# A graph-attention edge loop on one core: node parts and weights made two groups ahead, pairs weighed one pair ahead of TensorE

## The chip, the cores and the metric

The kernel runs on one core of a Trainium2 chip. The metric is the device time of one execution in microseconds, as the median of several runs without a profiler. Apart from these, one execution was recorded by the hardware profiler; all views come from that one.

## What is computed

Four graph layers on 4096 nodes with 512 features and 65536 edges (src, dst); each normalises, applies a relu, runs the layer and adds its result to x. The change lies in layer 0, a graph attention with 8 heads of 64 features:

```
h = einsum('nc,hcf->hnf', x, W)
e = s_src[:, :, None] + s_dst[:, None, :]
e = where(e > 0, e, 0.2 * e);  e = where(adj, e, NEG_INF)
att = softmax(e, axis=-1)
out = einsum('hij,hjf->hif', att, h)     # then softmax over the 512 features
```

adj has every edge once and the diagonal. The kernel doesn't build the 4096 x 4096 matrix. It goes over the edges, sorted by source: for each edge it gathers the destination's row of h (512 numbers) and 8 scores, makes a weight exp(...) for each of the 8 heads, and adds weight times row to the source node, together with the weight itself (the softmax's denominator) and a one (the degree, which layer 1 needs).

## The kernel before

**Stages.** The program sorts the edges and projects the nodes (to about 240 us of the profile), then runs layer 0's edge loop (`attend`), layer 1's edge loop (rows of ytab, from about 1190 us), layer 2's edge network (about 2080 to 4670 us), a node update, and layer 3's edge loop (rows of ztab, from about 5190 us). The three plain edge loops each issue 512 indirect gathers of 128 rows from GpSimd's queue (L412).

**A group.** `attend` works on 64 groups of 8 tiles of 128 edges. For a group g these are the steps, with the engine that runs them:

- `fetch` (GpSimd, L412): 8 indirect gathers into `rows[g]`, which has four buffers. The first gather of group g+3 waits until the sums of group g-1 have left its buffer.
- `one_hots` (DVE, L407): a 128 x 128 matrix for each tile that says which source node (within a window) an edge belongs to.
- `turn` (TensorE, L623): the 8 one-hots transposed into PSUM (`t_ps`).
- `turned` (ACT L631, two casts to bfloat16; ACT L635 and DVE L636, which blend the node parts of the two node blocks of the window into `of`). The blocks' numbers are read into registers by L418 first, on ACT's and on DVE's queue.
- `source_parts` (TensorE, L644): 8 small products that give each edge its source's part of the score (`e_ps`, a single buffer).
- `scores` (DVE L650, L652, L653, L654, L656: sum of three parts, add the gathered part, leaky relu, subtract the source's own top, clamp; ACT L657 exp and L658 ones).
- `weights` (DVE L664: weight times a mark that drops repeated edges, into PSUM `w_ps`, two buffers; ACT L665 copies it beside the rows).
- `weigh_last` (ACT L672): the last two heads of two tiles are scaled, four instructions for a pair of tiles.
- `weigh` (DVE L678): the first six heads of a pair of tiles, one instruction.
- `add_up` (TensorE, L684): a pair of tiles summed into `sum_ps`; four matmuls of 261 columns, which the profile shows as eight.
- `keep` (DVE L424, twice): the window's sums added into the accumulators of two node blocks, whose numbers also come through L418.

**What sets the order.** The loop stands under a manual schedule: each engine executes in the order in which the code names its instructions, and waits where data or a buffer is missing. So the order of the calls in the loop (L693 to L728) is the order on each queue. In iteration g the sums of group g are made, group g-1 is kept, group g+1 is turned, scored and weighted, the one-hots of g+2 are made and the rows of g+3 fetched. Within iteration g a pair of tiles is weighed on DVE just ahead of its sums: pair 0, sums 0, pair 2, (keep g-1), sums 2, pair 4, one-hots, sums 4, scores of g+1, pair 6, sums 6, weights of g+1.

Of the kernel before, what the change touches and what calls it, by code (L numbers as in the profile page):

```python
# [34 lines left out]
def kernel(  # L35
# [71 lines left out]
    s_loc = src_pool.tile([P, W], F32, name="s_loc")  # L107
# [296 lines left out]
    def one_hots(pool, loc, t0, n, bufs=None, ids=None, dtype=F32):  # L404

        oh = pool.tile([P, n, P], dtype, name="oh", bufs=bufs)
        nc.vector.tensor_tensor(oh, (row_i if ids is None else ids).unsqueeze(1).to_broadcast([P, n, P]),  # L407
                                loc[:, t0:t0 + n].unsqueeze(2).to_broadcast([P, n, P]), op=OP.is_equal)
        return oh
# [7 lines left out]
    def block_of(eng, bi, t):  # L417
        return eng.value_load(bi[:, t:t + 1], min_val=0, max_val=NB - 1)  # L418
# [171 lines left out]
    GT = 8  # L590
# [4 lines left out]
    def attend(ctx):  # L595
        if True:
            ep = ctx.enter_context(tc.tile_pool(name="edge", bufs=2))
# [4 lines left out]
            ids_ps = both_ps[:, :P]  # L602
# [5 lines left out]
            def at(g):  # L608
                return g * GT

            def fetch(g):
                rows = ep.tile([P, GT, DA], F32, name="rows", bufs=4)
                for j in range(GT):
                    gather(rows[:, j, :D + H], htab, s_dst[:, at(g) + j:at(g) + j + 1])
                return rows

            def turn(oh):

                made = []
                for j in range(0, GT, 4):  # L620
                    t_ps = eps.tile([P, 4, P], F32, name="t_ps")
                    for k in range(4):
                        nc.tensor.transpose(t_ps[:, k, :], oh[:, j + k, :], ident)  # L623
                    made.append(t_ps)
                return made

            def turned(g, made):

                oh_t = ep.tile([P, GT, P], BF16, name="oh_t")
                for j, t_ps in enumerate(made):  # L630
                    nc.scalar.copy(oh_t[:, 4 * j:4 * j + 4, :], t_ps)  # L631
                of = ep.tile([P, 2, 3 * 2 * H], BF16, name="of")
                near = [node3[:, ds(block_of(e, s_bi[:, k, :], g), 1)].rearrange("p b k c -> p (b k c)")
                        for k, e in enumerate((nc.scalar, nc.vector))]
                nc.scalar.activation(of[:, 0, :], near[0], AF.Copy, scale=s_half[:, 0, g:g + 1])  # L635
                nc.vector.scalar_tensor_tensor(of[:, 1, :], near[1], s_half[:, 1, g:g + 1], of[:, 0, :],  # L636
                                               op0=OP.mult, op1=OP.add)
                return oh_t, of[:, 1, :]

            def source_parts(oh_t, of):  # L640

                e_ps = eps.tile([P, GT, 3, 2 * H], F32, name="e_ps", bufs=1)
                for j in range(GT):
                    nc.tensor.matmul(e_ps[:, j].rearrange("p k c -> p (k c)"), oh_t[:, j, :],  # L644
                                     of, start=True, stop=True)
                return e_ps

            def scores(rows, e_ps):
                near = ep.tile([P, GT, 2 * H], F32, name="near")
                nc.vector.reduce_sum(near, e_ps.rearrange("p t k c -> p t c k"), axis=AX.X)  # L650
                u = ep.tile([P, GT, H], F32, name="u")
                nc.vector.tensor_add(u, near[:, :, :H], rows[:, :, D:D + H])  # L652
                nc.vector.scalar_tensor_tensor(u, u, 0.2, u, op0=OP.mult, op1=OP.max)  # L653
                nc.vector.tensor_sub(u, u, near[:, :, H:])  # L654

                nc.vector.tensor_scalar(u, u, SAFE_RANGE + 10.0, None, op0=OP.min)  # L656
                nc.scalar.activation(u, u, AF.Exp)  # L657
                nc.scalar.copy(rows[:, :, D + H:], one2.unsqueeze(1).to_broadcast([P, GT, 2]))  # L658
                return u

            def weights(g, rows, u):

                w = w_ps[:, g % 2]
                nc.vector.tensor_mul(w, u, s_new[:, at(g):at(g) + GT].unsqueeze(2).to_broadcast([P, GT, H]))  # L664
                nc.scalar.copy(rows[:, :, D:D + H], w)  # L665

            def weigh_last(j, rows):

                two = rows[:, j:j + 2]
                for k in range(2):  # L670
                    for h in range(VH, H):
                        nc.scalar.activation(two[:, k, h * F:(h + 1) * F], two[:, k, h * F:(h + 1) * F], AF.Copy,  # L672
                                             scale=two[:, k, D + h:D + h + 1])

            def weigh(g, j, rows):

                part = rows[:, j:j + 2, :VH * F].rearrange("p t (h f) -> p t h f", h=VH)
                nc.vector.tensor_mul(part, part,  # L678
                                     w_ps[:, g % 2, j:j + 2, :VH].unsqueeze(3).to_broadcast([P, 2, VH, F]))

            def add_up(j, rows, oh, ps):
                for k in range(2):
                    for c in range(2):
                        nc.tensor.matmul(ps[:, c, :HW], oh[:, j + k, :], rows[:, j + k, c * HW:(c + 1) * HW],  # L684
                                         start=j + k == 0, stop=j + k == GT - 1)

            def keep(g, ps):
                add_window(g, s_bi, s_half,
                           lambda b: acc[:, ds(b, 1), :].rearrange("p b (c d) -> p (b c) d", c=2), ps[:, :, :HW])


            rows, ohs, sums = {}, {}, {}
            for g in range(-3, groups + 1):  # L693
                now = lambda k: 0 <= k < groups
                if now(g + 3):
                    rows[g + 3] = fetch(g + 3)
                if now(g + 1):
                    made = turn(ohs[g + 1])
                if now(g):
                    sums[g] = eps.tile([P, 2, D], F32, name="sum_ps")  # L700
                    weigh(g, 0, rows[g])
                    add_up(0, rows[g], ohs[g], sums[g])
                    weigh_last(2, rows[g])
                    weigh(g, 2, rows[g])
                if now(g - 1):
                    keep(g - 1, sums.pop(g - 1))
                    del rows[g - 1], ohs[g - 1]
                if now(g + 1):
                    parts = turned(g + 1, made)
                if now(g):  # L710
                    add_up(2, rows[g], ohs[g], sums[g])
                    weigh_last(4, rows[g])
                    weigh(g, 4, rows[g])
                if now(g + 2):
                    ohs[g + 2] = one_hots(ep, s_loc, at(g + 2), GT, 3, ids_ps)
                if now(g + 1):
                    e_ps = source_parts(*parts)
                if now(g):
                    add_up(4, rows[g], ohs[g], sums[g])
                if now(g + 1):  # L720
                    u = scores(rows[g + 1], e_ps)
                if now(g):
                    weigh_last(6, rows[g])
                    weigh(g, 6, rows[g])
                    add_up(6, rows[g], ohs[g], sums[g])
                if now(g + 1):
                    weights(g + 1, rows[g + 1], u)
                    weigh_last(0, rows[g + 1])  # L728

    one2 = node_pool.tile([P, 2], F32, name="one2")  # L730
    nc.vector.memset(one2, 1.0)
    attend()
    l0_pool.close()

# [734 lines left out]
```

## Time and profile before

| | |
|---|---|
| median of 3 runs (lowest to highest) | 5614.41 us (5613.85 to 5614.54) |
| the profiled execution's own time | 5951.3 us |
| its span, first to last instruction | 5949.5 us |
| mean granted TensorE clock | 0.951 |
| busy in the span: PE, DVE, ACT, POOL | 88%, 60%, 56%, 52% |
| layer 0's loop, 240 to 1030 us, busy: PE, DVE, ACT, POOL | 600.5, 519.7, 366.5, 484.1 of 790 us |
| in the same stretch: TensorE clock, share of DMA engines | 0.92, 0.63 |

How to read it: times in the profile are microseconds from the first instruction. PE is TensorE's matmuls, whose ends are modelled; DVE is VectorE, ACT ScalarE, POOL GpSimd. An idle time is put down to what ended it, as far as the profile can name it. Indirect gathers show as DMA_INDIRECT on POOL; [...] the rows land later.

### The profile page before, as it was taken

The numbers are of one execution on the slowest core, as the hardware profiler recorded it, in microseconds if no ns is written. First come the engines' busy times: TensorE is split into PE (matmuls) and PEld (weight loads), VectorE is DVE, ScalarE is ACT, GpSimd is POOL, SyncE is SP. The second block draws the span as 40 slices with busy tenths as digits, with TensorE's granted clock in tenths as the row PEclk, the third lists the DMA queues.
The fourth block names the chain that finished last, engine by engine and source line by source line (L and its number), as shares of the span: only waits on it lengthen the run. The fifth ranks groups of instructions, "written<-read, shape, count | busy, mean of one in ns | idle before, by whom it ended". The sixth has DMA issues, their size and how long they took to land.

```text
span 5949.5 us, 56469 instructions
## 1 busy us (share of the span) xinstructions
PE 5249.2 (88%) x17274; PEld 2791.2 (47%) x17274; DVE 3558.3 (60%) x5695; ACT 3356.1 (56%) x5015; POOL 3082.0 (52%) x2604
## 2 busy tenths in 40 slices
PE   7677777869999799999999999999999899866676
PEld 4466666424444344444444444444444666522222
DVE  8566667623223377777777777777777565522323
ACT  1144445423433488888888888888888433333333
POOL 0266664066666465665565566566554111166665
PEclk9799999989999899999999999999999999988888
DMA  3366665467777555555555555555554212266775
GB/s 105 98 176 181 184 181 159 159 212 232 234 227 232 147 118 108 111 110 109 110 111 110 108 113 109 108 112 110 108 110 84 78 64 68 84 187 187 209 222 183
DMA packets 344871, 841.72 MB, mean 141 GB/s; under 512 B 60272, under 2 KB 76656, under 8 KB 344560
## 3 DMA queue, kind: packets, MB, share of 16 engines
q0 software_dynamic: 237568, 673.35, 46.8%
q1 hardware_dynamic: 106992, 164.66, 8.1%
q8 instruction: 141, 2.31, 0.2%
q14 instruction: 170, 1.39, 0.1%
HBM read 752.62 MB, written 85.20 MB: 141 GB/s over the span
## 4 chain that ended last, share of the span: by engine, by line
PE 75%; DVE 8%; another core or an unknown queue 6%; issue 4%; ACT 3%; DMA 2%; DVEq 1%; POOL 1%; SPq 0%; POOLq 0%; ACTq 0%
PE m_ps L401 30%; PE sum_ps L768 13%; PE small_ps L967 5%; PE tr_ps L974 4%; PE sum_ps L994 4%; PE pq_ps L868 4%; PE o_ps L401 4%; PE u_ps L1177 4%; PE sum_ps L684 4%; DVE rows L678 2%; DVE acc L424 1%; PE y_ps L401 1%; ACT oh L744 1%; POOL rows L412 1%
## 5 line engine op out<-in xcount | busy, mean ns | idle before, releaser
L401 PE MATMUL m_ps<-w_sb,h_t 128*128 128x512 f32 x4096 | 1848.0, 599 | 1.5 <-ACT h_t L976 1.5
L768 PE MATMUL sum_ps<-g,oh 128*128 128x512 f32 x2048 | 1012.2, 636 | 248.2 <-ACT oh L745 133.1
L401 PEld LDWEIGHTS m_ps<-w_sb,h_t 128*128 128x128 f32 x4096 | 757.1, 190 | 1002.9 <-issue 989.1
L950 POOL DMA_INDIRECT pg<-qtab,d_dst x512 | 1050.9, 2053 | 156.5 <-issue 155.4
L412 POOL DMA_INDIRECT pg<-ptab,d_src x512 | 498.5, 974 | 909.6 <-ACT h_t L976 726.4
L768 PEld LDWEIGHTS sum_ps<-g,oh 128*128 128x128 f32 x2048 | 412.1, 205 | 793.6 <-issue 600.2
L412 POOL DMA_INDIRECT rows<-htab,s_dst x512 | 484.1, 946 | 515.8 <-issue 360.1
L424 DVE SCALAR_TENSOR_TENSOR acc<-sum_ps,d_half,acc 128x512 f32 x512 | 384.6, 751 | 581.8 <-remote 241.3
L412 POOL DMA_INDIRECT g<-ytab,s_dst x512 | 484.9, 947 | 460.8 <-issue 326.9
L684 PE MATMUL sum_ps<-rows,oh 128*128 128x261 f32 x2048 | 528.2, 408 | 160.2 <-DVE rows L678 87.1
L412 POOL DMA_INDIRECT g<-ztab,d_src x512 | 486.6, 950 | 324.5 <-issue 142.7
L424 DVE SCALAR_TENSOR_TENSOR acc<-sum_ps,s_half,acc 128x522 f32 (+1 forms) x256 | 193.6, 756 | 575.1 <-PE sum_ps L768 275.7
L684 PEld LDWEIGHTS sum_ps<-rows,oh 128*128 128x128 f32 x2048 | 392.5, 199 | 249.5 <-DVE rows L678 101.1
L976 ACT COPY h_t<-tr_ps 128x512 f32<-128x512 f32 x512 | 287.2, 588 | 338.8 <-PE tr_ps L974 314.2
L994 PE MATMUL sum_ps<-parts,oh 128*128 128x512 f32 x1024 | 344.1, 457 | 12.4 <-DVE parts L987 10.7
L868 PE MATMUL pq_ps<-w_sb,ht_mid 128*128 128x512 f32 x512 | 272.2, 619 | 58.7 <-ACT ht_mid L863 58.7
L988 DVE TENSOR_TENSOR parts<-z,parts 128x1024 fp32r<-128x1024 f32 x256 | 313.9, 1226 | 8.7
L967 PE MATMUL small_ps<-w1e,et 64*128 64x512 f32 x1024 | 295.3, 648 | 20.8 <-ACT et L959 13.0
L744 ACT ACTIVATE oh<-row_i,d_loc 128x128 f32<-128x128 f32 x512 | 162.2, 387 | 249.5 <-remote 149.1
L974 PE MATMUL tr_ps<-ident,pg 128*128 128x128 f32 x2048 | 297.4, 278 | 3.9 <-DVE pg L1070 0.6
L974 PEld LDWEIGHTS tr_ps<-ident,pg 128*128 128x128 f32 x2048 | 224.6, 142 | 118.7 <-issue 84.5
L1168 POOL TENSOR_TENSOR h_sb<-h_sb,b_bc 128x1024 f32<-128x1024 f32 x16 | 37.7, 2357 | 453.5 <-PE tr L1152 358.0
(283 smaller groups left out, 7937.7 us busy)
## 6 DMA issues: line engine op xcount, KB each, us to landing
xt<-in_x_dram SPq DMA_DIRECT2D x16, 1024.0 KB
eg<-in_edge_attr_dram SPq DMA_DIRECT2D x128, 128.0 KB
htab<-acc SPq DMA_DIRECT2D x32, 256.0 KB
rows<-htab,s_dst POOLq DMA_INDIRECT x512
x<-xt SPq DMA_DIRECT2D x8, 1024.0 KB
ytab<-acc SPq DMA_DIRECT2D x32, 256.0 KB
x_mid<-x SPq DMA_DIRECT2D x32, 256.0 KB
g<-ytab,s_dst POOLq DMA_INDIRECT x512
```

What stands on the lines that cost most here:

```text
L401: nc.tensor.matmul(ps, h_t[:, k, :], w_sb[:, k0 + k, :], start=start and k == 0, stop=stop and k == KC - 1)
L412: nc.gpsimd.indirect_dma_start(out=dst_ap, out_offset=None, in_=table, in_offset=bass.IndirectOffsetOnAxis(ap=idx, axis=0))
L424: nc.vector.scalar_tensor_tensor(at, ps, half[:, k, i:i + 1], at, op0=OP.mult, op1=OP.add)
L684: nc.tensor.matmul(ps[:, c, :HW], oh[:, j + k, :], rows[:, j + k, c * HW:(c + 1) * HW], start=j + k == 0, stop=j + k == GT - 1)
L768: nc.tensor.matmul(ps, oh[:, j, :], g[:, j, :], start=i % per == 0 and j == 0, stop=i % per == per - 1 and j == U - 1)
L868: nc.tensor.matmul(ps, h_t[:, k, :], self.w1_sb[:, k0 + k, :], start=k == 0, stop=k == KC - 1)
L950: nc.gpsimd.indirect_dma_start(out=pg[:, j, :], out_offset=None, in_=qtab, in_offset=bass.IndirectOffsetOnAxis(ap=d_dst[:, t:t + 1], axis= ...
L967: nc.tensor.matmul(ps, et[half, j // 2, :], w1e[half, :], start=True, stop=True)
L974: nc.tensor.transpose(h_ps[:, k, :], h[:, j, k * P:(k + 1) * P], ident)
L976: nc.scalar.copy(h_t, h_ps)
L988: nc.vector.tensor_sub(parts[:, 1], m, parts[:, 0].bitcast(F32))
L994: nc.tensor.matmul(ps, oh[:, j, :], parts[j // 2][:, k, j % 2, :], start=j == 0 and k == 0, stop=j == U - 1 and k == 1)
```

## The change

Only the loop of `attend` is changed. Turning, blending, scores and weights now belong to group g+2 in iteration g, not g+1; the one-hots to g+3, with four buffers instead of three. A pair of tiles is weighed one pair ahead of its sums: pair 0 of the next group at the end of an iteration, pair 2 right after the sums of pair 0 are issued, and so on. `keep` of the group before stands after `turned`, ahead of the weighing of pair 6, and the weights follow the scores directly at the end of the iteration. No instruction is added or removed in a group, and `fetch` stays where it was. The order on the queues is then, in iteration g:

- DVE: pair 2, pair 4, L636 (g+2), keep (g-1), pair 6, pair 0 (g+1), one-hots (g+3), scores (g+2), L664 (g+2)
- ACT: L672 for pair 2 and 4, casts and L635 (g+2), L672 for pair 6 and for pair 0 (g+1), exp, ones and L665 (g+2)
- TensorE: sums 0, transposes (g+2), sums 2, sums 4, source parts (g+2), sums 6

```diff
@@ -694,38 +694,37 @@
                 now = lambda k: 0 <= k < groups
                 if now(g + 3):
                     rows[g + 3] = fetch(g + 3)
-                if now(g + 1):
-                    made = turn(ohs[g + 1])
                 if now(g):
                     sums[g] = eps.tile([P, 2, D], F32, name="sum_ps")
-                    weigh(g, 0, rows[g])
                     add_up(0, rows[g], ohs[g], sums[g])
                     weigh_last(2, rows[g])
                     weigh(g, 2, rows[g])
+                if now(g + 2):
+                    made = turn(ohs[g + 2])
+                if now(g):
+                    weigh_last(4, rows[g])
+                    weigh(g, 4, rows[g])
+                    add_up(2, rows[g], ohs[g], sums[g])
+                if now(g + 2):
+                    parts = turned(g + 2, made)
                 if now(g - 1):
                     keep(g - 1, sums.pop(g - 1))
                     del rows[g - 1], ohs[g - 1]
-                if now(g + 1):
-                    parts = turned(g + 1, made)
-                if now(g):
-                    add_up(2, rows[g], ohs[g], sums[g])
-                    weigh_last(4, rows[g])
-                    weigh(g, 4, rows[g])
-                if now(g + 2):
-                    ohs[g + 2] = one_hots(ep, s_loc, at(g + 2), GT, 3, ids_ps)
-                if now(g + 1):
-                    e_ps = source_parts(*parts)
-                if now(g):
-                    add_up(4, rows[g], ohs[g], sums[g])
-                if now(g + 1):
-                    u = scores(rows[g + 1], e_ps)
                 if now(g):
                     weigh_last(6, rows[g])
                     weigh(g, 6, rows[g])
+                    add_up(4, rows[g], ohs[g], sums[g])
+                if now(g + 2):
+                    e_ps = source_parts(*parts)
+                if now(g):
                     add_up(6, rows[g], ohs[g], sums[g])
                 if now(g + 1):
-                    weights(g + 1, rows[g + 1], u)
                     weigh_last(0, rows[g + 1])
+                    weigh(g + 1, 0, rows[g + 1])
+                if now(g + 3):
+                    ohs[g + 3] = one_hots(ep, s_loc, at(g + 3), GT, 4, ids_ps)
+                if now(g + 2):
+                    weights(g + 2, rows[g + 2], scores(rows[g + 2], e_ps))
 
     one2 = node_pool.tile([P, 2], F32, name="one2")
     nc.vector.memset(one2, 1.0)
```

## The prediction

> **What bounds the kernel now.** I read, in this order, the page (layer 0's loop over edges is L684/L678/L672), the waits between 260 and 1020 us, the timelines of DVE, ACT and PE in two stretches of that loop, and every indirect gather (L412) of the program. The loop runs from the first gather at 240.4 us to the end of the last keep at 1029.9 us, 64 groups. The waits (who waited, for whom: us, times, longest):
> ```profile
> ACT oh_t L631 <- remote: 84.4, 36, 7.1
> ...
> DVE acc L424 <- remote: 77.8, 34, 3.1
> ...
> POOL rows L412 <- remote: 70.3, 34, 2.1
> DVE acc L424 <- PE t_ps L623: 53.8, 25, 2.4
> ```
> Three engines wait once in nearly every group, and all for TensorE ("remote" is a releaser that the profile could not name; the same waits end at the transposes L623 in other groups). One group on DVE (start, length, what, idle before):
> ```profile
> 603.08 1.58 DVE L424 SCALAR_TENSOR_TENSOR acc<-sum_ps,s_half,acc 128x522 f32 x2 [2.17 <-remote]
> 604.70 0.27 DVE L636 SCALAR_TENSOR_TENSOR of<-node,s_half,of 128x48 bf16<-128x48 bf16 x1
> 604.89 0.95 DVE L678 TENSOR_TENSOR rows<-rows,both_ps 128x768 f32<-128x768 f32 x1
> 605.75 1.22 DVE L407 TENSOR_TENSOR oh<-both_ps,s_loc 128x1024 f32<-128x1024 f32 x1
> 607.56 0.56 DVE L650 TENSOR_REDUCE near<-e_ps 128x128 f32<-128x384 f32 x1 [0.59 <-PE sum_ps L684]
> 608.15 0.23 DVE L652 TENSOR_TENSOR u<-near,rows 128x64 f32<-128x64 f32 x1
> ...
> 608.93 0.35 DVE L656 TENSOR_SCALAR u<-u 128x64 f32<-128x64 f32 x1
> 609.04 0.95 DVE L678 TENSOR_TENSOR rows<-rows,both_ps 128x768 f32<-128x768 f32 x1
> 610.09 0.23 DVE L664 TENSOR_TENSOR both_ps<-u,s_new 128x64 f32<-128x64 f32 x1
> 610.76 1.82 DVE L678 TENSOR_TENSOR rows<-rows,both_ps 128x768 f32<-128x768 f32 x2 [0.43 <-issue]
> 614.83 1.57 DVE L424 SCALAR_TENSOR_TENSOR acc<-sum_ps,s_half,acc 128x522 f32 x2 [2.25 <-PE t_ps L623]
> ```
> The keep pair (L424) recurs every 11.75 us (603.08, 614.83, 626.58). Its sums' last matmul started at 600.00, and yet it is released at 603.08. Now the last groups, when no gather is left, first TensorE, then DVE:
> ```profile
> 1010.00 2.03 PE L684 MATMUL sum_ps<-rows,oh 128*128 128x261 f32 x8 [1.12 <-DVE rows L678]
> 1011.87 1.04 PE L623 MATMUL t_ps<-ident,oh 128*128 128x128 f32 x8
> ...
> 1019.16 6.00 PE L684 MATMUL sum_ps<-rows,oh 128*128 128x261 f32 x26 [0.66 <-DVE rows L678]
> ```
> ```profile
> 1012.30 1.55 DVE L424 SCALAR_TENSOR_TENSOR acc<-sum_ps,s_half,acc 128x522 f32 x2
> ```
> The same code goes round in 9.16 us (1010.00 to 1019.16), and keep starts 0.65 us after its last matmul instead of 3.1. So TensorE's work is not the bound; its word of completion comes 2 to 2.5 us late while gathers run. Is that lateness there when nobody profiles? The profiled execution took 5951.3 us (span 5949.5), the median is 5614.41: 336.9 less. The three gather stages of the program:
> ```profile
> L412 POOL DMA_INDIRECT rows<-htab,s_dst x512: 940/946/1119, 240.4 to 1000.7; - x171
> ```
> ```profile
> L412 POOL DMA_INDIRECT g<-ytab,s_dst x512: 940/946/1445, 1190.2 to 1956.8; - x171
> ```
> ```profile
> L412 POOL DMA_INDIRECT g<-ztab,d_src x512: 940/946/1430, 5193.1 to 5919.3; - x171
> ```
> One gather is 0.946 us and the next starts 0.30 later, 1.25 each; 511 x 1.25 = 638.8. First to last start took 760.3, 766.6 and 726.2: over POOL's pace by 121.5 + 127.8 + 87.4 = 336.7. That is the whole 336.9. I take it that in the timed runs POOL paces these stages without a stop: in layer 0 that is 8 x 1.25 = **10.0 us a group**, above the 9.16 that the rest needs. It is an inference from one equality; layer 2's loop can hardly hold the difference: TensorE is busy 2573.8 of the 2590 us from 2080 on.
>
> [...] in the trace, a register load of keep (L418) starts only when the wait ahead of it is met.
>
> **The change part by part.** Every instruction of a group stays (no DMA is moved, fetch stays first, so POOL's and SP's queues are untouched); only order changes. [...]
>
> (1) Removed: the waits for late TensorE words. Keep (2.2 us), the casts L631 (2.1) and the reduction L650 (0.6) now come most of a group, or several us, after their matmuls. Under profile this is worth at most 11.75 - 10.0 = 1.75 a group. In the timed runs it is worth **nothing**: POOL's 10.0 hides it. If that cover is gone, the full cycle counts.
>
> (2) Added on DVE: the weights product (L664) now follows the clamp (L656) with no weighing between them. Clamp to exp 0.39 (608.93 to 609.32), exp 0.26, hop 0.04: 0.68 instead of 0.11. What is queued behind: the weighings of pairs 2 and 4.
>
> (3) Added on DVE and ACT: L636 must now run ahead of keep, the weighing of pair 6 and pair 0, the one-hots and the reduction, and it waits for ACT's L635. ACT gets there late: from the product's start, product 0.23, copy L665 0.19, hops 0.07, eight head scalings (L672, 2.02 for eight overlapped, 1.94 to the next start), two casts 0.96, L635 0.35, hop 0.04: 3.79 us. DVE has the two weighings in that time (1.74, plus 0.3 if the first waits for the copy), so it stands idle 1.6 to 1.8. TensorE's sums of pair 6 and, through them, POOL's next fetch wait for it.
>
> (4) Keep after L636: its register load can't start before L636's wait is met. Load 0.304, two register steps 0.183 and 0.099, an assert 0.023 and gaps: 0.80 to 0.83 (603.10 to 603.90 between the two keeps). Bounds: 0.19, if the load gets ahead anyway (10.5 in all), and 1.2, since one load took 1.1 at 1013.1. I take 0.83.
>
> The cycle from one L636 to the next: register load 0.83 + keep 1.60 + weighings of pair 6 and 0 at 0.87 each + one-hots 1.14 + reduction 0.59 + three score steps 0.78 + clamp to product 0.68 + product to L636 3.79 = **11.15 us**. It doesn't hang on TensorE's lateness: transposes start some 3 us before ACT can cast them. TensorE idles some 2 us before pair 6, so its half-clock windows (PEclk 0.93 in the loop) are mostly covered; I count nothing, up to 0.3 a group.
>
> Sum. Timed runs before: gathers 638.8 + landing 3.1 (begun at 603.3, landed at 606.4) + from the last group's reduction to its last keep 13.2 (1016.7 to 1029.9) = 655 us for the loop. After: first group landed at 7 x 1.25 + 3.1 = 12, and 64 x 11.15 = 714: 726. **+71 us: 5614.4 + 71 = 5685.** Against the profiled execution's own 5951.3 (1.8 of it around the span) the sign is the other: there the loop goes from 789 to some 740, with 0.1 a group for lateness that still shows, so I expect it to fall to 5900 to 5930 while the median rises.
>
> **Rivals.**
> *The lateness is real in every execution* (faster). Place: TensorE's completion to keep, L631, L650; price 11.75 - 9.16 = 2.6 a group. Then before is 11.75 and after 11.2: 64 x 0.5 = 32 less, **5582**. It decides once about three quarters of the lateness is there unprofiled (before above 11.15). For it: every profiled group shows it. Against: the 336.7.
> *After also reaches POOL's pace* (no change): loads run ahead and ACT's scalings fall elsewhere. The longer drain stays, since a group is scored two ahead: one group, 9 us: **5623**. Against: the order on ACT is fixed, L672 twice ahead of L631.
> *Slower with a shorter ring*: register load 0.19, 10.5 a group, 684 in all: **5645**. *With a longer one*: 1.2 and half-clock 0.3: 11.8, **5727**.
>
> **How the numbers follow.** Forecast ring near 11.15 (5660 to 5710): 0.50. Shorter ring 0.17, longer 0.11: slower, 0.78 together. POOL's pace kept, or partial lateness that cancels: 0.08 within 0.2% (5603 to 5626, about what a measurement can tell from no change). Lateness real: 0.14 faster. The range takes in the slower cases, up to 5730, and the no-change case, from 5602; outside lies faster and a little above. The slower cases' own range is 5640 to 5727.
>
> **What would show it.** Right: in the profile after, L424 recurs every 11.0 to 11.5 us; DVE L636 idles 1.5 us or more for ACT's L635, some 100 us in all; L664 waits about 0.5 for exp; L424 no longer waits for TensorE but 0.6 for issue; sums L684 wait about 2 us once a group for DVE's L678; POOL idles about 1 us a group; the gap between profiled time and median shrinks from 337 to some 230. Wrong: L424 every 10.0 us (the ring is shorter), or a median that falls with the profile (the lateness is real).

## The result and the profile after

| | before | after |
|---|---|---|
| median (lowest to highest), 4 runs each | 5614.48 us (5613.85 to 5614.77) | 5660.64 us (5659.55 to 5661.46) |
| ratio after / before, 95% interval | | 1.0082 [1.0065, 1.0100] |
| the profiled execution's own time, span | 5951.3, 5949.5 us | 5661.09, 5659.2 us |

The kernel became 46 us slower. The forecast had +71 us and the direction; but it also had a profiled execution of 5900 to 5930 us and a gap of some 230 us to the median, and that gap is under half a microsecond (after's profiled execution is also one of its four runs). One thing is needed for reading all numbers below: on one of the four chips of the experiments TensorE's completions (the release of an engine that waits for its result) come late while gathers run: in the kernel before with two more scalings on ACT (below), keep waits 138.1 us there in 60 waits (57.6 us of it put down to TensorE, the rest to a releaser that the profile could not name), 2.3 each, against 1.5 us in 2 waits in the kernel before on another chip. On the late chip the kernel before takes 5947.82 us without any profiler (31 runs), while on the three others, with prompt completions, it takes 5613 to 5615; the profile of before shown above looks like the first sort, the comparison in the table and the profile of after like the second, though the record names no chip for these.

The rows of the three gather stages after (line L412; shortest/median/longest in ns, first and last start in us):
```profile
L412 POOL DMA_INDIRECT rows<-htab,s_dst x512: 940/946/1119, 238.5 to 912.1; - x171
L412 POOL DMA_INDIRECT g<-ytab,s_dst x512: 940/946/1467, 1102.7 to 1764.6; - x171
```
The third (ztab) goes from 5001.2 to 5641.9. Layer 0's 673.6 us is 35 above 512 gathers at POOL's own pace (638.8). The 661.9 of ytab is 23 above it, but so it is in the kernel before on a prompt chip (661.7, below), and the third stage's 640.7 is at it. One group on DVE after, from one L636 to the next (start, length, what, idle before):
```profile
608.78 0.27 DVE L636 SCALAR_TENSOR_TENSOR of<-node,s_half,of 128x48 bf16<-128x48 bf16 x1 [1.28 <-ACT of L635]
609.59 1.59 DVE L424 SCALAR_TENSOR_TENSOR acc<-sum_ps,s_half,acc 128x522 f32 x2 [0.55 <-issue]
611.10 1.81 DVE L678 TENSOR_TENSOR rows<-rows,both_ps 128x768 f32<-128x768 f32 x2
612.82 1.22 DVE L407 TENSOR_TENSOR oh<-both_ps,s_loc 128x1024 f32<-128x1024 f32 x1
613.96 0.55 DVE L650 TENSOR_REDUCE near<-e_ps 128x128 f32<-128x384 f32 x1
614.54 0.22 DVE L652 TENSOR_TENSOR u<-near,rows 128x64 f32<-128x64 f32 x1
...
615.32 0.20 DVE L656 TENSOR_SCALAR u<-u 128x64 f32<-128x64 f32 x1
615.84 0.23 DVE L664 TENSOR_TENSOR both_ps<-u,s_new 128x64 f32<-128x64 f32 x1 [0.32 <-ACT u L657]
...
619.45 0.27 DVE L636 SCALAR_TENSOR_TENSOR of<-node,s_half,of 128x48 bf16<-128x48 bf16 x1 [1.28 <-ACT of L635]
```
The ring that the prediction drew is there (a closed chain of steps, here from DVE to ACT and back, in which each step waits for the one ahead of it, so that no group takes less than one round). It goes round in 619.45 - 608.78 = 10.67 us. No row of it waits for TensorE: keep (L424), which idled 2.2 us for it in the profile of before, now idles 0.55 for nothing but its own register load (L418, 0.304 us), which starts only when L636's wait is met: 12 to 14 ns after L636's start in the first 61 groups. In its place L636 idles 1.28 for ACT. What ACT does in the time before (the same view of ACT):
```profile
605.54 2.02 ACT L672 ACTIVATE rows<-rows 128x64 f32<-128x64 f32 x8
607.47 1.04 ACT L631 CAST oh_t<-t_ps 128x512 bf16<-128x512 f32 x2
608.41 0.34 ACT L635 ACTIVATE of<-node,s_half 128x48 bf16 x1
```
None of the three shows an idle time: ACT goes through eight scalings, two casts and the blend without a stop, and the blend is the last of them. The waits of the whole stretch 260 to 910 us (who, for whom: us in total, times, longest):
```profile
PE sum_ps L684 <- DVE rows L678: 124.9, 119, 4.3
DVE of L636 <- ACT of L635: 77.9, 61, 1.3
POOL rows L412 <- PE sum_ps L684: 49.6, 50, 1.4
DVE acc L424 <- issue: 33.9, 60, 0.9
DVE both_ps L664 <- ACT u L657: 19.6, 61, 0.3
DVE rows L678 <- ACT rows L665: 17.2, 61, 0.3
```
Read from below: DVE waits for ACT three times a group (for the copy L665, for exp, and longest for the blend) and for its register load once, TensorE's sums wait 124.9 / 61 = 2.05 us a group for DVE, and POOL, whose next rows need the buffer that these sums release, waits about once a group for TensorE. POOL has lost its place as the slowest.

### The profile page after: what moved, and what is told of

The parts are those of the page before. It is cut to its first block, busy times and chain, and to the rows that moved or that the text cites. A ratio compares the mean times of both kernels' runs of the same rounds, so it can differ in the third digit from the quotient of the medians.

```text
span 5659.2 us, 56468 instructions
## 1 busy us (share of the span) xinstructions
PE 5206.5 (92%) x17274; PEld 2718.4 (48%) x17274; DVE 3554.4 (63%) x5695; ACT 3351.2 (59%) x5015; POOL 3083.9 (54%) x2604
## 4 chain that ended last, share of the span: by engine, by line
PE 68%; DMA 6%; POOL 4%; issue 2%; ACT 1%; DVE 1%; DVEq 0%; SPq 0%; POOLq 0%; ACTq 0%
PE m_ps L401 32%; PE sum_ps L767 9%; DMA g<-ztab,d_src 5%; PE small_ps L966 5%; PE tr_ps L973 4%; PE sum_ps L993 4%; PE o_ps L401 4%; PE u_ps L1176 4%; PE pq_ps L867 4%; POOL g L412 4%; PE tr L1151 1%; PE y_ps L401 1%; PE tr_ps L956 0%; ACT h_t L1153 0%; PE turn_mid L860 0%
## 5 line engine op out<-in xcount | busy, mean ns | idle before, releaser
L767 PE MATMUL sum_ps<-g,oh 128*128 128x512 f32 x2048 | 1027.4, 618 | 131.1 <-DMA g<-ztab,d_src 84.6
L412 POOL DMA_INDIRECT pg<-ptab,d_src x512 | 498.8, 974 | 909.4 <-ACT h_t L975 726.1
L412 POOL DMA_INDIRECT rows<-htab,s_dst x512 | 484.2, 946 | 427.1 <-DMA nodes<-node 236.8
L767 PEld LDWEIGHTS sum_ps<-g,oh 128*128 128x128 f32 x2048 | 357.5, 191 | 740.8 <-issue 339.5
L424 DVE SCALAR_TENSOR_TENSOR acc<-sum_ps,d_half,acc 128x512 f32 x512 | 384.7, 751 | 482.6 <-PE sum_ps L767 404.5
L412 POOL DMA_INDIRECT g<-ytab,s_dst x512 | 486.8, 951 | 364.9 <-DMA x_mid<-x 189.6
L412 POOL DMA_INDIRECT g<-ztab,d_src x512 | 485.9, 949 | 239.8 <-issue 117.6
L684 PE MATMUL sum_ps<-rows,oh 128*128 128x261 f32 x2048 | 488.7, 391 | 129.2 <-DVE rows L678 129.2
L684 PEld LDWEIGHTS sum_ps<-rows,oh 128*128 128x128 f32 x2048 | 380.0, 190 | 208.1 <-DVE rows L678 150.8
L424 DVE SCALAR_TENSOR_TENSOR acc<-sum_ps,s_half,acc 128x522 f32 (+1 forms) x256 | 193.6, 756 | 408.2 <-PE sum_ps L767 336.6
L1167 POOL TENSOR_TENSOR h_sb<-h_sb,b_bc 128x1024 f32<-128x1024 f32 x16 | 38.1, 2382 | 453.3 <-PE tr L1151 334.4
L1052 DVE TENSOR_TENSOR z<-m_ps,b_bc 128x512 f32<-128x512 f32 x128 | 88.6, 692 | 301.8 <-PE m_ps L401 301.8
```

Source lines behind the costliest of these rows:

```text
L412: nc.gpsimd.indirect_dma_start(out=dst_ap, out_offset=None, in_=table, in_offset=bass.IndirectOffsetOnAxis(ap=idx, axis=0))
L424: nc.vector.scalar_tensor_tensor(at, ps, half[:, k, i:i + 1], at, op0=OP.mult, op1=OP.add)
L767: nc.tensor.matmul(ps, oh[:, j, :], g[:, j, :], start=i % per == 0 and j == 0, stop=i % per == per - 1 and j == U - 1)
```

## The experiments

"Loop" is the time from the first gather of layer 0 to the end of its last keep; "ring" is the median distance from keep to keep. The first four of these kernels, with before itself as the first, ran on one prompt chip, where before takes 5615.0 us (23 runs).

**The kernel before, unchanged, once more.** 

> The kernel before, unchanged, profiled once more. If POOL paces its loop in the timed runs (the theory), and if the late completions of TensorE belonged to that one profiled execution, this profile spans some 5613 us, the 512 gathers of layer 0 go from first to last start in 639 to 645 us, and the keep pair recurs every 10.0 us. If the lateness is part of the kernel, the span is again near 5950 and keep recurs every 11.75 us.

Measured: 5620.66 us in its one, profiled run. Two rows, of the gathers (as above) and of the waits between 260 and 870 us:
```profile
L412 POOL DMA_INDIRECT rows<-htab,s_dst x512: 945/949/1123, 241.3 to 882.3; - x171
```
```profile
DVE u L652 <- DMA rows<-htab,s_dst: 49.6, 53, 2.2
```
Here is a profiled execution without the lateness. The gathers take 641.0 us, 2 us above POOL's own pace; the ring is 10.02 and the loop 658.5. In 53 of these groups DVE waits for gathered rows. So POOL paces the kernel before, and the reading holds for profiled and timed runs alike on this chip.

**Keep ahead of the blend.** In after, keep stands behind L636; here it goes first, all else stays:
```diff
-                if now(g + 2):
-                    parts = turned(g + 2, made)
                 if now(g - 1):
                     keep(g - 1, sums.pop(g - 1))
                     del rows[g - 1], ohs[g - 1]
+                if now(g + 2):
+                    parts = turned(g + 2, made)
```


> The changed kernel with keep ahead of turned, so that its register loads and its two additions fall into DVE's wait for ACT. Ring theory: product to L636 stays about 3.6 but keep (1.5) and its load (0.81) leave the ring, which becomes about 8.8 us, below POOL's 10.0. The loop is POOL-paced again: 5614 to 5625 (a longer drain, one group at most, stays). Rival, the loss comes from looking two groups ahead (gathered rows needed a group earlier, longer drain, buffers): the order of keep changes little, 5650 to 5661.

Measured: 5618.52 us (12 runs, 5614.63 to 5623.21), ratio to before 1.0007 [0.9998, 1.0016]; ring 10.00, loop 660.0. DVE in one group:
```profile
603.26 1.82 DVE L678 TENSOR_TENSOR rows<-rows,both_ps 128x768 f32<-128x768 f32 x2 [0.28 <-ACT rows L665]
605.00 1.55 DVE L424 SCALAR_TENSOR_TENSOR acc<-sum_ps,s_half,acc 128x522 f32 x2
606.59 0.27 DVE L636 SCALAR_TENSOR_TENSOR of<-node,s_half,of 128x48 bf16<-128x48 bf16 x1
...
611.40 0.23 DVE L652 TENSOR_TENSOR u<-near,rows 128x64 f32<-128x64 f32 x1 [1.21 <-DMA rows<-htab,s_dst]
```
Keep's work now fills the time in which DVE stood waiting for ACT, its register load is hidden, and the 1.2 us that come free end up in a wait for gathered rows: POOL paces again. One swap of two calls gives back some 42 of the 46 us.

**ACT's part of the blend first.** The other half of the ring: the casts and L635 move ahead of the scalings of pair 4 on ACT, and DVE's order stays as in after.
```diff
-            def turned(g, made):
+            def turned_act(g, made):
...
+            def turned_dve(g, oh_t, of):
...
                 if now(g + 2):
-                    made = turn(ohs[g + 2])
+                    half = turned_act(g + 2, turn(ohs[g + 2]))
...
                 if now(g + 2):
-                    parts = turned(g + 2, made)
+                    parts = turned_dve(g + 2, *half)
```


> The changed kernel with only ACT's order changed: the two casts and L635 ahead of the head scalings of pair 4 (four L672). Ring theory: product to L636 falls from 3.61 by 0.96 to about 2.65, the ring from 10.67 to 9.7, below POOL's 10.0: 5614 to 5625. Rival, looking two groups ahead is the cost in itself: 5650 to 5661, since nothing of that changes.

Measured: 5618.46 us (12 runs, 5615.21 to 5621.72), ratio 1.0007 [0.9999, 1.0016]; ring 9.96, loop 660.0. The wait of after's L636 (here L640, 260 to 870 us):
```profile
DVE of L640 <- ACT of L634: 20.0, 61, 0.4
```
It falls from 77.9 to 20.0 us (61 waits, 0.33 each); keep still stands behind it and still pays its load (34.0 us). Shortening the ring at either place is enough, because only some 0.7 us of it lies above POOL's 10.0. That speaks against the rival that looking two groups ahead costs something by itself in every group: both kernels look two groups ahead.

**Two of eight gathers taken away, kernel before.** Tiles 6 and 7 of each group get fixed rows by a plain DMA from SyncE, so that POOL needs only 6 x 1.25 = 7.5 us a group.
```diff
-                    gather(rows[:, j, :D + H], htab, s_dst[:, at(g) + j:at(g) + j + 1])
+                    if j < 6:
+                        gather(rows[:, j, :D + H], htab, s_dst[:, at(g) + j:at(g) + j + 1])
+                    else:
+                        nc.sync.dma_start(rows[:, j, :D + H], htab[:P, :])
```


> The kernel before with 6 indirect gathers a group; the rows of tiles 6 and 7 come by a plain DMA of the table's first 128 rows on the SP queue (so the rows of these tiles are not the edges' own). Bytes are the same, POOL has 7.5 us a group. If POOL paces before, the loop falls to its own ring of 9.16 us: 64 x 0.84 = 54 us less, about 5560. If POOL does not pace it (its own ring or data does), it stays at 5605 to 5614.

Measured: 5567.11 us (4 runs), ratio 0.9915 [0.9899, 0.9932]; ring 9.23, loop 606.5; some 7 us above the 5560 that was expected. POOL now stops once a group (start, length, what, idle before):
```profile
608.62 0.95 POOL L412 DMA_INDIRECT rows<-htab,s_dst  x1 [2.14 <-PE sum_ps L687]
```
Take POOL's pace away and before falls by 48 us, to a ring of its own of 9.23, close to the 9.16 that the prediction read from the last groups.

**The same in after, and in after with keep first.** These two and the next two ran on a chip with late completions, where before takes 5947.82 us; their medians are compared only with one another and with that.

> The changed kernel with 6 indirect gathers a group, tiles 6 and 7 by a plain DMA of the table's first 128 rows (their rows are not the edges' own). Ring theory: POOL had slack of about 0.7 us a group already, so nothing moves: 5655 to 5661, keep again every 10.67 us. If gathers or their data pace the changed loop, it falls as the kernel before did, by some 50 us.

> The changed kernel with keep ahead of turned (as in the run before of that kind) and 6 indirect gathers a group, tiles 6 and 7 by a plain DMA of the table's first 128 rows (their rows are not the edges' own). Without POOL's floor the ring itself shows: 8.8 us, against the 9.16 of the kernel before under the same relief. So some 20 us below that kernel's 5567, less one group of longer drain: about 5552. If the look-ahead costs something of its own, it is not below 5567.

Measured: 5865.04 us (4 runs) for after with six gathers, 5772.81 (4 runs) with keep first as well; ratios to before 0.9866 [0.9849, 0.9882] and 0.9702 [0.9686, 0.9718]. Rings 10.67 and 9.13, loops 707.6 and 613.1. The 5655 to 5661 and 5552 that were expected rest on the times of a prompt chip, so these medians say nothing of them; the ring of the second is above its 8.8. DVE in the first of them (L639 is after's L636, shifted by the added lines):
```profile
605.36 0.27 DVE L639 SCALAR_TENSOR_TENSOR of<-node,s_half,of 128x48 bf16<-128x48 bf16 x1 [1.28 <-ACT of L638]
```
The wait is 1.28 and the ring 10.67, both to the hundredth those of after with eight gathers on the other chip: with a quarter of POOL's work gone nothing in after's ring moves. It doesn't hang on POOL. (That the loop is 707.6 and not 702.5 comes ahead of the first keep, 44.6 us after the first gather instead of 39.0.) The swap of keep shortens it here too.

The last of these on a chip with prompt completions (before 5614.5 us there, 7 runs):

> The changed kernel with keep ahead of turned and 6 indirect gathers a group, tiles 6 and 7 by a plain DMA of the table's first 128 rows (their rows are not the edges' own). With prompt completions the reduction no longer waits (0.27 us a group on the other chip, ring 9.13): ring 8.8 to 8.9 against 9.23 of the kernel before under the same relief, 5545 to 5558 against its 5567. With late completions: 5773 again. If the look-ahead costs something of its own beyond POOL's floor, not below 5567.

Measured: 5547.0 us (4 runs, 5542.58 to 5551.23), ratio 0.9877 [0.9861, 0.9894]; ring 8.93, loop 588.0. It is 20 us below the kernel before with the same six gathers (5567.11, another chip, with before at 5615.0). So the look-ahead with keep first does shorten the ring, 8.93 against 9.23, and with all eight gathers POOL's 10.0 covers both.

**Two more scalings on ACT.** A doubled cost: two idle copies of 64 columns in each group ahead of the casts, in before and in after; results go nowhere.
```diff
                 oh_t = ep.tile([P, GT, P], BF16, name="oh_t")
+                for j in range(2):
+                    idle = ep.tile([P, F], F32, name="idle")
+                    nc.scalar.activation(idle, row_i[:, :F], AF.Copy, scale=s_half[:, 0, g:g + 1])
```


> The kernel before with two more 128x64 scalings on ACT (0.24 us each, result unused) ahead of the casts in each group. Ring theory: ACT is not in the way of POOL's 10.0 (the own ring is 9.16, at most 9.65 with them): within 3 us of before. A theory in which ACT's time or the ring paces the kernel before: up to 31 us more.

> The changed kernel with the same two scalings on ACT ahead of the casts. Ring theory: they lie on the ring between product and L636, 64 x 0.48 = 31 us more: 5689 to 5693, and L636 idles 1.76 instead of 1.28. If the ring does not run through ACT, they hide in its idle time (4.9 us before exp) and it stays at 5660.

Measured, still on the chip with late completions: in before 5947.93 us (12 runs), ratio 0.9994 [0.9985, 1.0003], nothing; in after 5955.39 (20 runs), ratio 1.0015 [1.0009, 1.0022], ring 11.88, loop 799.3. DVE in one group of the second:
```profile
611.98 0.56 DVE L653 TENSOR_REDUCE near<-e_ps 128x128 f32<-128x384 f32 x1 [0.84 <-PE sum_ps L687]
...
617.95 0.27 DVE L639 SCALAR_TENSOR_TENSOR of<-node,s_half,of 128x48 bf16<-128x48 bf16 x1 [1.76 <-ACT oh_t L634]
```
The wait for ACT has grown by 0.48, from 1.28 to 1.76, and in this group the reduction waits 0.84 for TensorE's source parts, which the prompt chip doesn't show. Over the loop (260 to 1010 us):
```profile
DVE near L653 <- PE sum_ps L687: 38.7, 56, 1.5
```
That is 0.69 each; 10.67 + 0.48 + 0.69 is 11.84, and the median ring is 11.88. So the change doesn't free the ring of lateness altogether: on DVE only a keep, two weighings and the one-hots stand between the source parts and their reduction.

The same kernel and after itself on a chip with prompt completions (before 5613.36 us there, 7 runs), and after once more on a third (before 5614.5):

> The changed kernel itself. Two chips have shown themselves: on one, completions of TensorE are prompt (the kernel before takes 5615 us), on the other they come late while gathers run (the kernel before takes 5948 us, also in timed runs, keep every 11.77 us). Where they are prompt: 5660 and keep every 10.67 us, as before. Where they are late: the order of the change hides part of it, and the ring has 3 us between the source parts and the reduction that needs them; 10.67 to 11.4 us a group, the loop 710 to 755 instead of 785 to 790, so 30 to 75 us less than before: 5875 to 5920, faster than before. If lateness cancels the change altogether, equal to before within 10 us.

> The changed kernel with two more scalings of 0.24 us on ACT ahead of the casts, again. Ring theory: 64 x 0.48 = 31 us more than the changed kernel on the same chip, L636 idles 1.76 us instead of 1.28. Prompt completions: 5689 to 5693, keep every 11.15 us. Late ones: keep near 11.9 and about 5955 again. If the scalings are not on the ring: no more than the changed kernel on the same chip.

> The changed kernel once more, for a chip on which TensorE's completions come late (the kernel before takes 5948 us there). On such a chip: keep every 10.7 to 11.9 us instead of 11.77, so at most 60 us faster than before and at most 5 us slower; the theory of the ring takes no side closer than that, since how late the source parts' completion comes has only been seen with two scalings more (ring 11.9). On a chip with prompt completions: 5660 to 5663 again.

Measured: after 5662.7 us and 5660.82 us (4 runs each), ratios 1.0089 [1.0072, 1.0106] and 1.0081 [1.0064, 1.0098], rings 10.67 and 10.68: the result again. With two more scalings 5686.65 us (4 runs, 5685.94 to 5691.1), ratio to before 1.0134 [1.0117, 1.0151]; ring 11.15, loop 731.3. Its waits, 260 to 910 us:
```profile
DVE of L639 <- ACT of L638: 101.8, 58, 1.8
```
Now 1.75 for each of the 58. ACT's 0.48 goes into the ring to the hundredth, 10.67 to 11.15, and the median rises by 24 to 26 us. That is short of the 29 to 33 us expected (5689 to 5693): the loop itself is 29 us longer than in after on that chip (731.3 against 702.2), and why the whole program grows by less stays open. In these rings ACT's work ahead of L635 is paid in full. Before took the same work for nothing, though that was seen on the other chip alone, where POOL is not the pace.

None of the kernels here that do all the gathers beats before.

## Why the prediction was right or wrong

**Direction and mechanism: right.** That POOL's 10.0 us a group leaves a shorter ring nothing to gain was shown twice: by the undisturbed profile of before (ring 10.02) and by taking gathers away (9.23). Of the three waits that the change removes, though, there was little left for POOL to hide in a timed run. In that undisturbed profile (260 to 870 us) only the reduction still waits in every group, 0.43 us each:
```profile
DVE near L650 <- PE e_ps L644: 25.8, 60, 1.2
ACT oh_t L631 <- PE t_ps L623: 4.0, 5, 1.6
DVE acc L424 <- PE sum_ps L684: 1.5, 2, 1.0
```
That the new ring runs L636, keep's load, weighings, scores, product, ACT, L636 was shown by breaking it at keep and at ACT (10.00 and 9.96), by lengthening it (10.67 to 11.15) and by taking POOL out of it (still 10.67).

**The step that failed: lateness only where a profiler runs.** The prediction took the equality of 336.7 us of slow gathers and 336.9 us between profiled time and median as showing that TensorE's completions are late under the profiler alone. The repeated profile of before has no lateness, and before without a profiler takes 5947.82 us on another chip (31 runs), close to the 5951.3 of the profiled execution shown ahead of the change. The likely reading is that the median and the profile came from two chips, since both times recur, each on chips of one sort; the record names no chip for either, and as each chip was measured in one stretch of time, a condition of the moment is not ruled out. Nor was the equality as exact as it looked: in the undisturbed profile layer 1's gathers still take 661.7 us, 23 above POOL's pace. Against that profile, the first loop of the profile shown ahead of the change is longer by 131 us (789.5 - 658.5), the next two gather stages by 105 and 84, and some 12 come after the last gather. The conclusion for the timed runs stood, since these show none of the lateness; everything said on the profiled execution (5900 to 5930 us, a gap of 230) fell with the step. The rival that the step displaced, "the lateness is real in every execution", was nearer to the truth on such a chip, but the timed runs of the comparison don't show it, and its 5582 did not come.

**The size: the terms of the ring.** 11.15 was forecast, 10.67 measured:

| term | forecast | measured |
|---|---|---|
| L636 to keep (register load) | 0.83 | 0.81 |
| keep to weighing | 1.60 | 1.51 |
| two weighings | 0.87 + 0.87 | 0.86 + 0.86 |
| one-hots, reduction, three score steps | 1.14 + 0.59 + 0.78 | 1.14 + 0.58 + 0.78 |
| clamp to product | 0.68 | 0.52 |
| product to L636 | 3.79 | 3.61 |

0.34 of the 0.48 lie in the two hand-overs between DVE and ACT. The clamp took 0.35 in the group of before that was read and takes 0.20 here. And ACT's first scaling does not wait for the end of the copy L665: it starts 0.10 after the copy's start (605.44 and 605.54), where the copy and a hop had been counted in full. Keep's 0.09 is the rest of it, beside small change. The register load, whose bounds were widest (0.19 to 1.2), came within 0.02. So the rival with the shorter ring (10.5), to which 10.67 is nearer than to 11.15, was not right for its reason, a load of 0.19. The half-clock windows, which the author's estimate put at up to 0.3 a group, did not come: from 260 to 910 us after's granted clock is 1.00, where before's profile has stretches at 0.50 (611.9 to 612.4 us; the matmuls of L684 take 642 ns there, 383 at full clock).

Some of the recorded sums are loose by rounding: the terms for 3.79 add up to 3.78 and those for 0.68 to 0.69, and the rivals' 5645 and 5582 come out 1 to 3 us lower. The landing of a gather, put at 3.1, is 3.3 at the least and 3.8 in the median over after's gathers. None of this decides anything.

The other terms of the sum: before's loop 655 against 658.5 measured, after's 12 + 64 x 11.15 = 726 against 702.5. With the ring at 10.67 that formula would give 695; the pipeline, one group deeper, starts later than the formula has it. Counted from the keeps, with after and before side by side: first gather to first keep 39.0 and 27.2 us (+11.8); 61 distances of 10.66 and 10.03 (+38.1); the last two distances 11.9 and 17.9 (-6.0). Together +44, against a rise of the median of 46. With keep first the start costs +9.2, the distances -1.7 and the end -6.0: that is the +1.5 of its loop (660.0 against 658.5), so the deeper start nearly pays for itself in the shorter end. The prediction's rival at POOL's pace had set one whole group, 9 us, for it (5623; measured 5618.5, with no change inside its interval).

**What would show it.** Right: L424 no longer waits for TensorE and idles some 0.6 for issue, sums wait 2 us a group for L678 (1.41 and 0.59), POOL waits about once a group. Off: L424 recurs every 10.67 us, outside the 11.0 to 11.5 that were named, and the median lies at the very edge of the 5660 to 5710 given to this ring; the forecast ring has the right steps and is 0.48 too long. L636 idles 1.28, not 1.5 or more, because of the two short terms and because the weighing of pair 2 also waits 0.28 for the copy; L664 waits 0.32, not 0.5; POOL idles 0.7 more than its pace, not 1.

**What stays open.** Where completions come late, the change itself was never timed: each of its runs fell on a prompt chip. Before's ring is 11.77 (median) in the profile shown ahead of the change, and on the late chip after with 0.48 us more per group is slower by 7.6 us only; so after without them may well gain, as the forecast said of the profiled execution. That is argued, not shown. Nor is it known why completions come late there. The granted clock, which is lower in those executions (0.951 against 0.98), does not account for it: in the profile of before, 33 of the 54 middle groups had the full clock from the last sum to its keep, and there the keep came 3.14 us after that sum's start; on a prompt chip it is 0.65 (kernel before once more: eight matmuls from 597.20 for 2.04 us, as long as at full clock, and keep at 599.50).

## What to carry to other kernels

Before a wait is removed, find the engine whose own pace sets the loop: here, with prompt completions, POOL's 8 x 1.25 us covered the waits on DVE, ACT and TensorE, and a new order had nothing to win. Where the order of an engine's queue is fixed, as by the manual schedule here, put work that is ready (keep) ahead of work that waits for another engine (L636), above all work with a register load: behind L636 it cost 0.81 us a group, ahead of it nothing. And when a profile and the timed median differ by per cents, take the profile again before building a theory on the gap: the two profiled executions of the kernel before took 5951.3 and 5620.66 us.

## What the runs showed of the hardware

- On one of four chips TensorE's completions come late while gathers run: keep waits 2.3 us in 60 groups of the kernel before with two more scalings. Before is 5947.82 us there without the profiler and 5613 to 5615 on the three others. In the profile of before that shows the same wait, keep starts 3.14 us after the start of the last sum, on a prompt chip 0.65.
- How late they come differs within that chip. In after with six gathers of eight the word of the sums was prompt in layer 0 (POOL was released 2.3 us after the start of the sums it waits for, 598.01 to 600.32, as in after on a prompt chip, 601.43 to 603.74), while of layer 1's gathers in the same execution only 334 fell between 1200 and 1700 us, as in the late profile of before (334), against 386 in after. With keep first and six gathers the sums' word was prompt as well (2.3 us, 603.82 to 606.11), but the reduction still waited 0.28 us a group for the source parts, for which it doesn't wait on a prompt chip (no wait of the reduction from 260 to 870 us). Which of the gathers, their number or the order makes the difference was not separated.
- Small scalings on ACT cost the ring their share: two more of 64 columns took 0.48 us (ring 10.67 to 11.15), where eight in a row take 1.93 (605.54 to 607.47).
